# A graph-attention kernel, first layer: key tiles made of 64 keys from each of two chunks

## The chip, the cores and the metric

The kernel runs on one core of a Trainium2 chip. The metric is the time on the device in microseconds (us). Engines are named as in the profile: PE is TensorE's matmul, PEld its weight load, DVE is VectorE, ACT is ScalarE, POOL is GpSimd, SP is SyncE, which here only issues DMAs.

## The reference

Eight inputs `x[b]` of 2048 rows by 256 features pass through two layers, all in f32, with one `adj` of 2048 x 2048 for all. Each layer normalises `x`, applies a ReLU to get `h`, and adds its result to `x`. The first layer is the one that is changed:

```python
q = (h @ Wq.T + bq).reshape(B, N, H, Dh).transpose(0, 2, 1, 3)      # H = 4 heads, Dh = 64
...
kc = k.reshape(B, H, Nc, CHUNK, Dh)                                  # Nc = 8 chunks of 256 keys
vc = v.reshape(B, H, Nc, CHUNK, Dh)
scores = jnp.einsum('bhnd,bhjcd->bhnjc', q, kc) / sqrt(Dh)
scores = jnp.clip(scores, -10.0, 10.0)
scores = jnp.where(mask == 0, -10.0, scores)
attn = softmax(scores, axis=-1)                                      # within each chunk of 256 keys
ctx = jnp.einsum('bhnjc,bhjcd->bhnd', attn, vc)                      # the chunks' contexts are added
out = ctx @ Wo.T + bo
out = layernorm(out + h) * gamma + beta
```

What matters: the softmax is taken within each chunk of 256 keys. A chunk's weights are divided by their own sum before the contexts of the eight chunks are added. The second layer is another attention over the same rows, with scores `e_src[i] + e_dst[j]` and one softmax over all 2048 keys.

## The kernel before, in words

**Steps.** The first layer is a written-out sequence of 256 steps: 8 inputs (`b`, called batches), 4 blocks of 512 queries (`qb`), 8 chunks of keys (`c`). A step handles all four heads of one chunk. Its 256 keys are two key tiles of 128 (`kt`), with keys on the partitions and queries along the free axis. The loop at the end of `layers` runs over `n` and works on three steps at once: contexts of step `n`, sums of step `n + 1`, scores of step `n + 2`. Instructions go to each engine in the order in which this Python code emits them, and each engine takes its queue in that order.

**What a step does.**

- `scores` (L436): for a key tile and a pair of heads (`hp`), two matmuls with 64 features on the rows and 128 keys on the columns write a pair of PSUM banks (`pair()`, three pairs in rotation, tile name `big`). DVE clips and masks them in one instruction (L449) into a weight tile `E` (ten of them in rotation). `exponential` (L455) on ACT makes the weights in place. There are four such tiles of 128 x 1024 per step.
- `added` in `prepared` (L776): POOL adds the two key tiles, once for each pair of heads, so that one matmul per head sums a chunk.
- `add_up` (L472): four matmuls with a 128 x 32 matrix of ones, 512 queries each, put each head's sums on 32 partitions. `divide` (L479) copies them on ACT; a DMA spreads them over 128 partitions (`got`). `spread` (L486) takes reciprocals on DVE and sends them through DRAM to `r` (L488, L491: one DMA to DRAM, four back, each for 32 partitions).
- `weigh` (L461): the contexts. Four heads stand beside each other as 128x32 tiles; a head's 64 features are two halves (`part`) in two PSUM banks (`both`). Both key tiles of the chunk accumulate there.
- `accumulate` (L499, L501): DVE multiplies each bank with `r` into `c`, or straight into `acc` for a query block's first chunk; POOL adds `c` to `acc`.

**Side work.** Beside the steps, generators do the rest. `batch` and `block` make the next input's keys, values and queries: `statistics` (L47, L48), `normal`, `turn` (L157), then `narrow` matmuls (L154). `limits` makes the masks from `adj` during the first batch. `finish` closes a query block once its eight chunks are in: output projection, residual (L535), second normalisation (L544, L553), storing. `advance` lets these generators go on at its place in a step, at most one matmul item per call; the numbers in `TURN` and in the dictionary in `block` say from which step on an item may go. A generator that yields `False` is not due yet. `finish` and `statistics` are in `quiet`, which only some calls of `advance` serve.

**PSUM.** The eight banks are three pairs, for scores, sums and side work alike, and the two banks of `both`. A score tile waits for a free pair, that is for the DVE instruction that read the pair's last content.

**After the first layer** the second one runs 512 rounds with its own loop (matmuls at L847 and L858, DVE at L837, POOL at L1060, ACT at L1019). Its work is not changed but for the order of keys within a block of 512. In its very last rounds `last_ending` (L914, L929, L930) does on DVE what `ending` (L977 to L986) does on ACT and POOL for all passes before.

Of the kernel before, what the change touches and what calls it, by code (L numbers as in the profile page):

```python
# [13 lines left out]
ALU = mybir.AluOpType  # L14
# [37 lines left out]
def layers(  # L52
# [99 lines left out]
    def narrow(to, lhsT, rhs, start, stop):  # L152
        for j in range(0, P, 32):
            nc.tensor.matmul(to[j : j + 32], lhsT[:, j : j + 32], rhs, start=start, stop=stop)  # L154
# [23 lines left out]
    def sides(rhs, two, hT):  # L178

        ps = aux().rearrange("p (t f) -> p t f", t=2)  # L180
        for u in range(2):
            t = 2 * two + u
            for ic in range(FC):
                narrow(
                    ps[:, u, :],
                    hT[:, ic, t * P : (t + 1) * P],
                    rhs[:, ic, :],
                    start=(ic == 0),
                    stop=(ic == FC - 1),
                )  # L190
        return ps
# [52 lines left out]

    def limits():
# [10 lines left out]
        def cast(k):  # L256

            m = masks[:, k % 2, :]
            nc.scalar.copy(m, raws[k])
# [30 lines left out]
    TURN = (1, NCH - 2, 2 * NCH - 2, 3 * NCH + 1)  # L290
# [5 lines left out]
    def block(b, blk, xb, turned, qs, ks, vs):  # L296

        def due(*slots):

            return b == 0 or here[0] >= first_of(b) + slots[blk]  # L300

        while not due(*TURN):
            yield False
        hT = big.tile([P, FC, QB], F32, tag="hT", name="hT", bufs=1)
        yield from block_turned(xb, blk, norm_of[b], hT)
# [3 lines left out]
        for name in ("qkv" if blk == 2 else "kvq"):  # L309
            while not due(*{  # L310
                "k": (0, 0, 3 * NCH - 1, 3 * NCH + 1),
                "v": (0, 0, 3 * NCH + 1, 3 * NCH + 3),
                "q": (NCH - 2, 2 * NCH - 2, 3 * NCH - 2, 4 * NCH - 2),
            }[name]):
                yield False
            if name == "v":
                r = big.tile([P, NT, F], F32, tag="kv", name="v", bufs=12)
                for two in range(NT // 2):
                    nc.scalar.copy(r[:, 2 * two : 2 * two + 2, :], sides(wT["v"], two, hT))
                    if two == 1:  # L320
                        vs.append(r)
                    yield
                continue
            if name == "q":
# [3 lines left out]
            for oc in range(FC):  # L328
                ps = aux()
# [15 lines left out]
    def batch(b):  # L345
# [11 lines left out]
        def statistics():  # L357

            for blk in range(NQB):
                while (  # L360
                    here[0] < first_of(b) + TURN[blk] - 2 or len(turned) < blk
                    if b
# [5 lines left out]
                yield from slot()  # L368
                for t in range(NT):
                    row_stats(nc, small, mv[:, blk * NT + t, :], xb[:, t, :])  # L370
# [16 lines left out]
    for name, w in (("q", Wq), ("k", Wk), ("v", Wv), ("o", Wo)):  # L387
# [4 lines left out]
        if name == "o":  # L392

            got = big.tile([P, FC, F], F32, tag="c", name="w_halves")
            for oc in range(FC):
                nc.vector.tensor_copy(
                    got[:, oc, :].rearrange("p (s h d) -> p h s d", s=2, h=H),
                    raw[:, oc, :].rearrange("p (h s d) -> p h s d", s=2, h=H),
                )
            raw = got  # L400
# [19 lines left out]
    for s in range(2):  # L420
        for h in range(H):
            f0 = h * DH + 32 * s
            nc.sync.dma_start(bv_col[32 * h : 32 * h + 32, s : s + 1], bv[f0 : f0 + 32].unsqueeze(1))
# [12 lines left out]
    def scores(qb, kt, hp, qs, ks):  # L436

        ps = pair()
        for hh in range(2):
            own = slice(hh * DH, (hh + 1) * DH)  # L440
            nc.tensor.matmul(  # L441
                ps[:, hh, :],
                ks[kt // NT][own, hp, (kt % NT) * P : (kt % NT + 1) * P],
                qs[qb][own, hp, :],
                start=True,
                stop=True,
            )
        e = weights_of.tile([P, 2, QB], F32, tag="E", name="E")
        nc.vector.scalar_tensor_tensor(  # L449
            e, ps, -0.5, bcast(limit[:, qb, kt, :], 1, 2), ALU.max, ALU.min  # L450
# [6 lines left out]
    def weigh(kt, part, es, vs, both, first):  # L457

        for h in range(H):
            mine = slice(h * DH + 32 * part, h * DH + 32 * part + 32)  # L460
            nc.tensor.matmul(  # L461
                both[part][32 * h : 32 * h + 32, :],
                vs[kt // NT][:, kt % NT, mine],
                es[h // 2][:, h % 2, :],
                start=first,
                stop=not first,
            )

    def add_up(es, sums):

        for h in range(H):
            nc.tensor.matmul(  # L472
                sums[32 * h : 32 * h + 32, :], ones, es[h // 2][:, h % 2, :], start=True, stop=True
            )

    def divide(sums):

        s = big.tile([P, QB], F32, tag="s", name="s", bufs=1)
        nc.scalar.copy(s, sums)  # L479
        got = small.tile([P, 16], F32, tag="sum", name="sum")  # L480
        nc.sync.dma_start(got, s[0:P:32, :].rearrange("h (j i) -> h j i", i=16))
        return got

    def spread(got):

        nc.vector.reciprocal(got, got)  # L486
        held = dram.tile([H, QB], F32, tag="inv", name="inv", bufs=3)
        nc.sync.dma_start(held.rearrange("h (j i) -> (h j) i", i=16), got)  # L488
        r = big.tile([P, QB], F32, tag="r", name="r", bufs=1)
        for h in range(H):  # L490
            nc.sync.dma_start(r[32 * h : 32 * h + 32, :], held[h, :].partition_broadcast(32))  # L491
# [881 lines left out]
```

## Time and profile before

Three runs took 4089.37, 4090.36 and 4090.54 us; the median is 4090.36 us.

| | us |
|---|---|
| median of three runs | 4090.36 |
| the profiled execution's own time | 4098.12 |
| its span, from the first to the last instruction | 4096.3 |
| busy in the span: PE | 3989.7 |
| POOL | 3287.0 |
| DVE | 3158.6 |
| ACT | 2517.7 |
| first copy of sums (L479) | 57.9 |
| last copy of sums | 2700.5 |
| first matmul of the second layer's contexts (L847) | 2731.0 |

The profile's page lists busy times, the chain of work that ended last, and the costliest groups of instructions: line, engine, operation, tile written from tiles read, partitions x elements, count, then total busy time in us and mean duration in ns, then the engine's idle time just before them and what ended it. In a timeline, each row has its start in us from the span's start, its length, engine, line and tiles; rows of one kind are merged, with their count. PE writes two records for one f32 matmul, so a count of 8 is four matmuls. The TensorE clock that the chip granted was 0.994 of the full one as a mean over the run.

### The profile page before, as it was taken

The page shows a single profiled execution, that of the slowest core. Times are in us where ns is not written, and L with a number is a line of the kernel's source. Part 1 is how long each engine was busy: PE and PEld are TensorE (multiplying, and loading weights), DVE is VectorE, ACT ScalarE, POOL GpSimd, SP SyncE. Part 2 cuts the span into 40 slices and gives each one's busy share as a digit, 9 for nine tenths or more (in the row PEclk, how much of TensorE's full clock was granted, in tenths as well). Part 3 has the DMA queues.
Part 4 walks back from the last instruction along what each step waited for, and adds up shares of the span by engine and source line. Part 5 has one row for each costly group of instructions (what it writes and reads, how often), then busy time and mean ns, then how long its engine had stood idle before and what let it go on. Part 6 is the DMA issues. An engine that isn't in the chain of part 4 may idle for free.

```text
span 4096.3 us, 85966 instructions
## 1 busy us (share of the span) xinstructions
PE 3989.7 (97%) x34614; PEld 1484.8 (36%) x34614; DVE 3158.6 (77%) x3500; ACT 2517.7 (61%) x3579; POOL 3287.0 (80%) x1828
## 2 busy tenths in 40 slices
PE   7999999999999999999999999989999999999997
PEld 3333333333333333333333333333333333333532
DVE  5786666676677677677666667759999999999998
ACT  5655556565555555655565556746676767767566
POOL 2577788788788888888888889868778788777887
PEclk9999999999999999999999999999999999999999
DMA  3221121111211121122112112222222222222221
GB/s 115 89 77 52 51 58 57 52 49 55 58 55 50 53 67 49 47 60 60 49 54 59 54 47 62 67 72 60 73 60 62 63 73 65 63 70 56 54 55 48
DMA packets 350344, 248.40 MB, mean 61 GB/s; under 512 B 232944, under 2 KB 300272, under 8 KB 349936
## 3 DMA queue, kind: packets, MB, share of 16 engines
q1 hardware_dynamic: 343664, 223.67, 20.0%
q0 software_dynamic: 5184, 18.88, 1.2%
q8 instruction: 274, 4.49, 0.5%
q14 instruction: 134, 1.10, 0.1%
q10 hardware_dynamic: 1088, 0.26, 0.0%
HBM read 204.15 MB, written 36.18 MB: 59 GB/s over the span
## 4 chain that ended last, share of the span: by engine, by line
PE 81%; POOL 8%; ACT 4%; DVE 3%; issue 2%; DMA 1%; SPq 0%; ACTq 0%; POOLq 0%; DVEq 0%
PE big L441 19%; PE acc L847 18%; PE both L461 17%; PE big L154 10%; PE big L472 7%; PE den L858 6%; PE rest L154 3%; POOL add L776 3%; POOL t L1060 3%; POOL acc L501 2%; ACT E L455 2%; DVE e L837 1%; PE big L157 1%; PE rest L157 1%; DMA sum<-s 1%
## 5 line engine op out<-in xcount | busy, mean ns | idle before, releaser
L449 DVE SCALAR_TENSOR_TENSOR E<-big,limit 128x1024 f32<-128x1024 f32 x1024 | 1181.9, 1217 | 642.2 <-PE big L441 614.6
L776 POOL TENSOR_TENSOR add<-E 128x1024 f32<-128x1024 f32 x512 | 1204.0, 2375 | 444.9 <-PE both L461 417.3
L455 ACT ACTIVATE E<-E 128x1024 f32<-128x1024 f32 x1024 | 1056.2, 1057 | 682.4 <-DVE E L449 664.2
L837 DVE SCALAR_TENSOR_TENSOR e<-near,far,limit 128x2048 f32<-128x2048 f32 x512 | 1166.4, 2345 | 25.0 <-issue 18.3
L1060 POOL TENSOR_TENSOR t<-t,e 128x1024 f32<-128x1024 f32 x384 | 905.6, 2394 | 210.3 <-PE den L858 100.1
L847 PE MATMUL acc<-e,qn 128*32 128x512 f32 x8192 | 983.2, 595 | 12.1 <-DVE e L837 11.8
L461 PE MATMUL both<-E,v 128*32 128x512 f32 x8192 | 992.6, 594 | 0.0
L441 PE MATMUL big<-qT,kT 64*128 64x512 f32 x4096 | 958.8, 605 | 14.6 <-DVE E L449 11.1
L441 PEld LDWEIGHTS big<-qT,kT 64*128 64x128 f32 x4096 | 365.1, 186 | 586.9 <-issue 416.7
L1019 ACT ACTIVATE t<-e,quot 128x1024 f32<-128x1024 f32 x384 | 420.7, 1144 | 215.0 <-PE den L858 147.6
L501 POOL TENSOR_TENSOR acc<-acc,c 128x1024 f32<-128x1024 f32 x224 | 531.2, 2371 | 6.2 <-DVE c L499 6.2
L461 PEld LDWEIGHTS both<-E,v 128*32 128x32 f32 x8192 | 294.4, 109 | 535.8 <-issue 396.7
L847 PEld LDWEIGHTS acc<-e,qn 128*32 128x32 f32 x8192 | 289.9, 110 | 539.1 <-issue 428.5
L499 DVE TENSOR_TENSOR c<-both,r 128x512 f32<-128x512 f32 x448 | 308.7, 690 | 43.7 <-PE both L461 10.4
L472 PE MATMUL big<-add,ones 128*32 128x512 f32 x2048 | 280.4, 602 | 15.7 <-POOL add L776 4.7
L858 PE MATMUL den<-t,for_sums 128*32 128x512 f32 x1536 | 229.5, 594 | 4.7 <-POOL t L1060 4.5
L479 ACT COPY s<-big 128x512 f32<-128x512 f32 x256 | 150.2, 587 | 77.0 <-PE big L472 76.9
L858 PE MATMUL den<-e,for_sums 128*32 128x512 f32 x1024 | 150.8, 592 | 0.0
L154 PE MATMUL big<-hT,wk 128*32 128x512 f32 x1024 | 124.9, 603 | 7.1 <-ACT hT L165 5.9
L472 PEld LDWEIGHTS big<-add,ones 128*32 128x32 f32 x2048 | 49.0, 107 | 224.9 <-issue 141.9
L977 ACT ACTIVATE z<-z,dens 128x64 f32<-128x64 f32 x496 | 125.3, 337 | 1.9 <-DVE z L961 1.9
L154 PE MATMUL big<-hT,wq 128*32 128x512 f32 x1024 | 125.2, 603 | 1.1 <-ACT hT L165 0.7
(144 smaller groups left out, 3126.9 us busy)
## 6 DMA issues: line engine op xcount, KB each, us to landing
r<-inv SPq DMA_DIRECT2D x1024, 64.0 KB
x<-in_x_dram SPq DMA_DIRECT2D x96, 512.0 KB
es<-er SPq DMA_DIRECT2D x64, 512.0 KB
adj_in<-in_adj_dram SPq DMA_DIRECT2D x32, 512.0 KB
x<-o POOLq DMA_DIRECT2D x32, 512.0 KB, 3.3
xh<-x SPq DMA_DIRECT2D x128, 128.0 KB
out_dram<-xh SPq DMA_DIRECT2D x124, 128.0 KB
x<-x SPq DMA_DIRECT2D x28, 512.0 KB
```

The lines of the kernel that those rows point to most:

```text
L154: nc.tensor.matmul(to[j : j + 32], lhsT[:, j : j + 32], rhs, start=start, stop=stop)
L441: nc.tensor.matmul(ps[:, hh, :], ks[kt // NT][own, hp, (kt % NT) * P : (kt % NT + 1) * P], qs[qb][own, hp, :], start=True, stop=True,)
L449: nc.vector.scalar_tensor_tensor(e, ps, -0.5, bcast(limit[:, qb, kt, :], 1, 2), ALU.max, ALU.min)
L455: nc.scalar.activation(e, e, AF.Exp, scale=0.25 * EDGE)
L461: nc.tensor.matmul(both[part][32 * h : 32 * h + 32, :], vs[kt // NT][:, kt % NT, mine], es[h // 2][:, h % 2, :], start=first, stop=not first,)
L472: nc.tensor.matmul(sums[32 * h : 32 * h + 32, :], ones, es[h // 2][:, h % 2, :], start=True, stop=True)
L501: nc.gpsimd.tensor_tensor(acc, acc, to, ALU.add)
L776: nc.gpsimd.tensor_tensor(both, tiles[0][hp], tiles[1][hp], ALU.add)
L837: nc.vector.scalar_tensor_tensor(e, near, far[:, jt, h : h + 1], limit[:, :, jt, :], ALU.max, ALU.min)
L847: nc.tensor.matmul(acc[part][32 * blk : 32 * blk + 32, :], qn[jt // NT][:, jt % NT, own], e[:, blk, :], start=(jt == 0), stop=(jt == NKT - 1),
L858: nc.tensor.matmul(den[32 * blk : 32 * blk + 32, :], for_sums[:, jt, :], blocks[blk], start=first, stop=last,)
L1060: nc.gpsimd.tensor_tensor(ts[half], ts[half], now[:, 2 * half : 2 * half + 2, :], ALU.add)
```

## The change

A step now handles two chunks (a block of 512 keys, `blk`) for one pair of heads (`hp`), instead of one chunk for four heads. There are still 256 steps. Key tile `t` of a block holds keys `64 t` to `64 t + 63` of the block's first chunk on partitions 0 to 63, and the same keys of its second chunk on partitions 64 to 127.

- Scores: four matmuls per tile of 64 features by 64 keys, instead of two of 64 by 128.
- Contexts: 64 keys by 64 features, one PSUM bank for each chunk, two heads beside each other, accumulated over four tiles.
- Sums: POOL adds the four tiles of a step with three instructions. One matmul for each head and each half of the queries (256 columns), with a matrix `both_of` that holds ones for either chunk in its own columns, gives the sums of both chunks.
- Reciprocals: `r` holds them for two chunks, 128 x 1024 instead of 128 x 512, brought by two DMAs of 64 partitions. It now takes turns with `c` in the same two buffers.
- `accumulate`: DVE multiplies each chunk's bank with its part of `r`, and DVE also adds the products to `acc`, in one instruction of 128 x 512 for each chunk (one in all in a query block's first two steps, two in the others). POOL's addition is gone.
- Order within a step: the context matmuls of the first tile stand ahead of the scores, those of the other three after them, then the sums. Both calls of `advance` stand at the end of a step.
- Side work: new times, one item for each step. `finish` is spread over 14 steps, `statistics` takes two tiles at a time, and the addition of the output bias comes after the projection.
- Values, masks, and the second layer's key order follow the new order of keys. The output weights are no longer reordered in halves.

The diff, cut to what the text speaks of:

```diff
+    def mixed(t):
+        return [256 * c + 64 * t + r for c in range(2) for r in (0, 32)]
...
-            nc.scalar.copy(m, raws[k])
+            nc.scalar.copy(
+                m.rearrange("p (b t c r) -> p b c t r", b=2, t=NT, c=2),
+                raws[k].rearrange("p (b c t r) -> p b c t r", b=2, c=2, t=NT),
+            )
...
-    TURN = (1, NCH - 2, 2 * NCH - 2, 3 * NCH + 1)
+    TURN = (3, NCH + 3, 2 * NCH + 3, 3 * NCH + 3)
+    ITEMS = {
+        "k": (5, NCH + 5, 2 * NCH + 7, 3 * NCH + 5),
+        "v": (7, NCH + 7, 3 * NCH + 1, 3 * NCH + 7),
+        "q": (9, NCH + 9, 2 * NCH + 5, 4 * NCH + 1),
+    }
...
-    def scores(qb, kt, hp, qs, ks):
+    both_of = const.tile([P, 32], F32, tag="both_of", name="both_of")
+    nc.gpsimd.memset(both_of, 0.0)
+    for c in range(2):
+        nc.gpsimd.memset(both_of[64 * c : 64 * c + 64, 16 * c : 16 * c + 16], 1.0)
+
+    def scores(qb, blk, t, hp, qs, ks):
         ps = pair()
-        for hh in range(2):
-            own = slice(hh * DH, (hh + 1) * DH)
-            nc.tensor.matmul(
-                ps[:, hh, :],
-                ks[kt // NT][own, hp, (kt % NT) * P : (kt % NT + 1) * P],
-                qs[qb][own, hp, :],
-                start=True,
-                stop=True,
-            )
+        for c in range(2):
+            for hh in range(2):
+                own = slice(hh * DH, (hh + 1) * DH)
+                keys = 256 * c + 64 * t
+                nc.tensor.matmul(
+                    ps[64 * c : 64 * c + 64, hh, :],
+                    ks[blk][own, hp, keys : keys + 64],
+                    qs[qb][own, hp, :],
+                    start=True,
+                    stop=True,
+                )
...
-    def weigh(kt, part, es, vs, both, first):
-        for h in range(H):
-            mine = slice(h * DH + 32 * part, h * DH + 32 * part + 32)
-            nc.tensor.matmul(
-                both[part][32 * h : 32 * h + 32, :],
-                vs[kt // NT][:, kt % NT, mine],
-                es[h // 2][:, h % 2, :],
...
+    def weigh(hp, t, e, v, both):
+        for hh in range(2):
+            mine = slice((2 * hp + hh) * DH, (2 * hp + hh + 1) * DH)
+            for c in range(2):
+                own = slice(64 * c, 64 * c + 64)
+                nc.tensor.matmul(
+                    both[c][64 * hh : 64 * hh + 64, :],
+                    v[own, t, mine],
+                    e[own, hh, :],
+                    start=(t == 0),
+                    stop=(t == NT - 1),
+                )
+    def add_up(added, sums):
+        for hh in range(2):
+            for half in range(2):
+                n = 2 * hh + half
+                nc.tensor.matmul(
+                    sums[32 * n : 32 * n + 32, :],
+                    both_of,
+                    added[:, hh, half * 256 : (half + 1) * 256],
+                    start=True,
+                    stop=True,
+                )
...
-        r = big.tile([P, QB], F32, tag="r", name="r", bufs=1)
-        for h in range(H):
-            nc.sync.dma_start(r[32 * h : 32 * h + 32, :], held[h, :].partition_broadcast(32))
+        r = big.tile([P, 2, 2, 256], F32, tag="c", name="r")
+        for hh in range(2):
+            nc.sync.dma_start(
+                r[64 * hh : 64 * hh + 64].rearrange("p n c q -> p (n c q)"),
+                held[4 * hh : 4 * hh + 4, :].rearrange("n q -> (n q)").partition_broadcast(64),
+            )
...
     def accumulate(acc, both, r, first):
-        to = acc if first else heads_tile("c", "c")
-        for part in range(2):
-            nc.vector.tensor_tensor(to[:, part, :], both[part], r, ALU.mult)
-        if not first:
-            nc.gpsimd.tensor_tensor(acc, acc, to, ALU.add)
+        to = big.tile([P, 2, QB], F32, tag="c", name="c")
+        parts = [acc if first and c == 0 else to[:, c, :] for c in range(2)]
+        for c, mine in enumerate(parts):
+            nc.vector.tensor_tensor(
+                mine.rearrange("p (n q) -> p n q", n=2),
+                both[c].rearrange("p (n q) -> p n q", n=2),
+                r[:, :, c, :],
+                ALU.mult,
+            )
+        for mine in parts[first:]:
+            nc.vector.tensor_tensor(acc, acc, mine, ALU.add)
...
+    def added(tiles):
+        total = heads_tile("add", "add")
+        nc.gpsimd.tensor_tensor(total, tiles[0], tiles[1], ALU.add)
+        for e in tiles[2:]:
+            nc.gpsimd.tensor_tensor(total, total, e, ALU.add)
+        return total
...
+    FIRST = 1
     for n in range(-2, len(steps)):
...
-            contexts(0)
-        if n < NQB * NCH or qb == NQB - 1 or qb == 0 and c < NCH // 2:
-            advance(n < 0)
-        coming = prepared(steps[n + 2]) if n + 2 < len(steps) else iter(())
-        weights[n + 2] = [next(coming, None)]
+            for t in range(FIRST):
+                weigh(hp, t, weights[n][t], v, both)
+        if n + 2 < len(steps):
+            weights[n + 2] = prepared(steps[n + 2])
+        if n >= 0:
+            for t in range(FIRST, NT):
+                weigh(hp, t, weights[n][t], v, both)
         inside = -1 <= n < len(steps) - 1
         if inside:
-            sums = pair()[:, 0, :]
-            add_up(weights[n + 1][1], sums)
+            sums = pair()[:, 0, :256]
+            add_up(totals.pop(n + 1), sums)
             got = divide(sums)
-        weights[n + 2].append(next(coming, None))
+        if n + 2 < len(steps):
+            totals[n + 2] = added(weights[n + 2])
         if n >= 0:
-            contexts(1)
...
-            accumulate(accs[qb], both, r, c == 0)
+            accumulate(accs[qb][:, hp, :], both, r, blk == 0)
...
             r = spread(got)
+        if n < 0 or b < B - 1 or qb == NQB - 1 or qb == 0 and c < NCH // 2:
+            advance(n < 0)
         advance(mask_first=0 <= n < NCH)
```

## The prediction

> **What bounds the kernel now.** I read the page first: the busy shares, the chain, then the groups of the first layer.
>
> ```profile
> PE 3989.7 (97%) x34614; PEld 1484.8 (36%) x34614; DVE 3158.6 (77%) x3500; ACT 2517.7 (61%) x3579; POOL 3287.0 (80%) x1828
> ...
> PE 81%; POOL 8%; ACT 4%; DVE 3%; issue 2%; DMA 1%; SPq 0%; ACTq 0%; POOLq 0%; DVEq 0%
> ...
> L449 DVE SCALAR_TENSOR_TENSOR E<-big,limit 128x1024 f32<-128x1024 f32 x1024 | 1181.9, 1217 | 642.2 <-PE big L441 614.6
> L776 POOL TENSOR_TENSOR add<-E 128x1024 f32<-128x1024 f32 x512 | 1204.0, 2375 | 444.9 <-PE both L461 417.3
> ...
> L501 POOL TENSOR_TENSOR acc<-acc,c 128x1024 f32<-128x1024 f32 x224 | 531.2, 2371 | 6.2 <-DVE c L499 6.2
> ...
> L499 DVE TENSOR_TENSOR c<-both,r 128x512 f32<-128x512 f32 x448 | 308.7, 690 | 43.7 <-PE both L461 10.4
> L472 PE MATMUL big<-add,ones 128*32 128x512 f32 x2048 | 280.4, 602 | 15.7 <-POOL add L776 4.7
> ```
>
> TensorE is the bound and owns 81% of the chain. But the first layer's POOL groups are big, and the change touches POOL and DVE. The copies of the sums (L479), one per step, stand at 57.9, 438.4, 2407.4 and 2700.5 us for steps 0, 32, 224 and 255. So a step takes 11.89 us in the first batch (masks are made there), 10.26 in the six middle ones, 9.46 in the last. In the windows of 1433.0 to 1757.9, 32 steps, PE is busy 322.62 us, POOL 276.58, DVE 225.50: per step 10.1, 8.64 and 7.05.
>
> The third view is the timeline, of one step and of the last 20 us.
>
> ```profile
> 1197.62 2.35 POOL L776 TENSOR_TENSOR add<-E 128x1024 f32<-128x1024 f32 x1
> 1199.15 4.62 DVE L449 SCALAR_TENSOR_TENSOR E<-big,limit 128x1024 f32<-128x1024 f32 x4 [0.98 <-PE big L441]
> 1200.41 2.19 ACT L455 ACTIVATE E<-E 128x1024 f32<-128x1024 f32 x2 [3.51 <-DVE E L449]
> 1201.65 1.06 PE L472 MATMUL big<-add,ones 128*32 128x512 f32 x8
> 1203.68 1.50 DVE L499 TENSOR_TENSOR c<-both,r 128x512 f32<-128x512 f32 x2
> 1204.22 1.94 PE L154 MATMUL big<-wv,hT 128*32 128x256 f32 x32
> 1204.52 4.72 POOL L776 TENSOR_TENSOR add<-E 128x1024 f32<-128x1024 f32 x2 [4.55 <-PE both L461]
> ...
> 4080.44 1.26 POOL L985 TENSOR_TENSOR z<-z,low 128x512 f32<-128x512 f32 x1
> 4081.01 2.91 DVE L914 TENSOR_TENSOR z<-z,dens 128x512 f32<-128x512 f32 x2
> 4081.78 1.59 POOL L986 TENSOR_TENSOR xh<-xh,z 128x512 f32<-128x512 f32 x1
> ```
> ```profile
> L914 DVE TENSOR_TENSOR z<-z,dens x2: 1239/1494/1748, 4081.0 to 4082.2; 128x512 f32<-128x512 f32 x2
> ...
> L930 DVE SCALAR_TENSOR_TENSOR xh<-xh,low x2: 692/692/692, 4085.7 to 4087.0; 128x512 f32<-128x512 f32 x2
> ```
>
> L914 decides this forecast. It is the only DVE work with both inputs in SBUF that runs beside POOL. Its first instruction ends at 4082.25, 0.55 after POOL's L985 (4081.70); its second at 4083.92, 0.55 after L986 (4083.37). L986, whose kind takes 1.26 to 1.29, took 1.59: it ended 1.12 after DVE's first. The two engines took turns, a whole instruction each. L930, also two SBUF inputs but with POOL idle, took 0.69.
>
> **The change part by part, per step.**
>
> *Sums on PE.* Four f32 matmuls over 512 columns (8 records, 1.06 us) become four over 256. L154 has that shape: 32 records in 1.94, so 8 take 0.49. Saved about 0.5 us, on the path while PE bounds: 256 x 0.5 = 128.
>
> *Scores and contexts as 64x64 tiles.* No row of before has that shape. The nearest: a pair of 64x128 takes 958.8/1024 = 0.94, a quad of 128x32 takes 992.6/1024 = 0.97. A step keeps four groups of each, so I take no change; were only two tiles at work at once, each group would double.
>
> *POOL.* Two adds become three: 3 x 2.36 = 7.1. The context addition leaves it (2.07 on average). With the finishing work (L553, L517, roots) it has 8.64 - 4.72 - 2.07 + 7.1 = 8.95 us: under any step below, if nothing holds it.
>
> *DVE.* Same four L449 (4.62) and two L499 (1.50), plus two additions into acc, one in the two steps of eight that start a block: 1.75 x 0.55 to 0.69. With reciprocal 0.25, statistics (384 pairs of 0.53 over 256 steps, 0.80) and L535 (0.17) this is 8.3 to 8.6 without waiting. But each addition reads acc and c, both in SBUF. Alone it costs 0.69 (L930), beside POOL 1.24 to 1.75 with POOL instructions of 1.26 (L914). POOL's here are 2.36 long, so the upper end is 2.36 + 0.55 = 2.9. Which end holds depends on what POOL does at that moment, so I lay out a step, time 0 at DVE's first L449:
>
> - L449 ends 4.62. The exponentials start 1.26 after it (1200.41 against 1199.15) and take 1.06 each at DVE's spacing: the second ends at 3.47. POOL starts 0.13 later: adds 3.60 to 5.96, 5.96 to 8.32, then the third.
> - PE: the fourth score tile needs the buffer that the first L449 frees (1.2); with it 2.1; three context groups of 0.86 (spacing in the chain of waits, 16 records in 1.72) end at 4.7. The multiplications run 4.9 to 6.4.
> - Addition one is issued at 6.4, into POOL's second add: waits to 8.32, ends 8.87. POOL's third add has been queued since 8.32, so it goes next: 8.87 to 11.23. Addition two: 11.23 to 11.78.
> - Reciprocal, statistics, L535: 1.22. The next L449 starts at 13.0.
>
> In the two steps with one addition it is 8.87 + 1.22 = 10.1. Mean (6 x 13.0 + 2 x 10.1)/8 = 12.3, over PE's 9.65 (10.15 less 0.5): DVE becomes the bound, through the waits. Queued behind the waiting addition are the reciprocal, with SyncE's inv and r DMAs and the x loads behind those, and the next L449, for which ACT's exponentials and PE's fourth score tile wait. r lands about 1.5 + 3.3 after the reciprocal (L488 to L491 is 1205.59 to 1207.03; 512 KB, twice the bytes of now, landed in 3.3 in the x<-o row): 3.8 into the next step, for a multiplication at 4.9. Hidden with 1.1 to spare.
>
> The Trainium skill's page "GPSIMD Engine Reference", section "Engine selection", sends elementwise additions to VectorE as about twice as fast. By that alone the move is a gain and the sum is that of the first rival. The page "SBUF — State Buffer", section "Who interferes with whom", speaks against the change: it says that a Vector instruction with two SBUF inputs contends with a GpSimd instruction that reads SBUF, whatever its form, where L914 shows one form, twice.
>
> *The rest.* Ten weight tiles now have to hold 3 + 4 + 4, so the fourth L449 also waits for the second context group: 2.1 + 0.86 = 3.0, before its turn at 3.46, so nothing. The statistics, turnings and projections are the same instructions in other steps; the 0.17 to 0.80 terms above carry them. x loads pass SyncE's r DMAs several steps ahead of their use: nothing. The mask cast writes 64-element runs (1.04 now, ACT 61% busy): nothing. Weight halves and seven small bv DMAs fall away at the start, under 1 us. The second layer, from about 2731 us on, keeps its work.
>
> **Sum**, against the profiled execution's 4098.1 (span 4096.3 and 1.8 around it; the median of runs is 7.8 lower). Middle batches: (12.3 - 10.26) x 192 = 392. First batch: the 24 mask parts left cost DVE 2.4 each, 1.8 per step: (12.3 + 1.8 - 11.89) x 32 = 71. Last, without x statistics: (12.3 - 0.2 - 9.46) x 31 = 82. Together +545: 4643, and 4635 as a median. I round to 4630.
>
> **The rivals.**
>
> *No waiting that counts (faster).* If the additions cost 0.55 to 0.69, DVE has 8.3 to 8.6 of 9.65, PE stays the bound and saves 128: 3965. For it: 30% of DVE is idle, and L914 is two instances. Against: each ends 0.55 after a POOL instruction. It decides as long as the waits stay below 9.65 - 8.4 = 1.25 us per step.
>
> *POOL holds the step.* DVE's waits are hidden, but each addition delays POOL by 0.55: 8.95 + 0.96 = 9.9 per step, (9.9 - 10.26) x 192 = -70, near 4020; up to 4080 if roots and additions bunch. Against: it needs the DVE waits gone and POOL's kept.
>
> *One whole POOL add is spared (slower, less).* Either DVE's second addition goes before POOL's queued third add (13.0 becomes 10.7), or the multiplications end before 5.96, so that addition one follows POOL's first add (11.2). The margin is only 6.4 - 5.96 = 0.44. Means 10.5 to 10.9, so 4190 to 4290.
>
> *64x64 tiles run two at a time.* 8 groups x 0.9 = 7 us more per step: about 5800. Against: the 64x128 pair and the 128x32 quad both fill the array in one group's time.
>
> **How the numbers follow.** Two waits 0.55 (4450 to 4830, the likeliest's own range); one spared 0.25; no waiting 0.12; POOL 0.05; two at a time 0.03. A difference under 0.2% is what a measurement of this kernel cannot tell from none. Faster: 0.12 and 0.02 of POOL's case, 0.14; same 0.03; slower 0.83. The range goes from 4150, below the spared case, to 4830; outside stand about 0.2.
>
> **What would show it.** Right: the two-input addition on DVE, x448, has a mean of 2 to 2.7 us and often ends 0.55 after a POOL add; POOL's x768 adds have a mean above 2.375, some near 2.9; PE's share falls to 85 to 88%; PE idles before score tiles, released by DVE's L449 successor; the sums group halves to about 140 us; steps alternate near 10 and 13. Wrong: additions below 1.2 us on average, or PE still at 97%. It would also be wrong, at another step, if the 64x64 groups' busy time left 960 to 990 us.

## The result, and the profile after

| | before | after |
|---|---|---|
| median of runs, us | 4090.43 | 4623.79 (4618.69 to 4627.06, four runs) |
| profiled execution's own time, us | 4098.12 | 4624.55 |
| its span, us | 4096.3 | 4622.7 |
| copies of the sums, first to last, us | 57.9 to 2700.5 | 58.6 to 3214.6 |
| mean granted TensorE clock | 0.994 | 0.960 |

The ratio of after to before is 1.1303, with a 95% interval of 1.1284 to 1.1323. The change makes the kernel 13% slower. The first layer carries it: from first to last copy of the sums 2642.6 us became 3156.0, +513.4 of the span's +526.4.

The profile's page of after: the busy shares, the chain of waits by engine, and the groups of the first layer. The lines of the kernel are now L461 for score matmuls, L469 for clipping, L483 for contexts, L496 for sums, L514 for reciprocals, L530 for multiplications, L537 for additions, L826 and L828 for POOL's adds.

```profile
PE 4068.4 (88%) x38710; PEld 1402.1 (30%) x38710; DVE 4070.4 (88%) x3946; ACT 2503.9 (54%) x3579; POOL 3496.8 (76%) x1863
...
PE 51%; DVE 23%; DMA 11%; issue 9%; POOL 3%; SPq 1%; ACT 1%; DVEq 0%; POOLq 0%; ACTq 0%
...
L461 PE MATMUL big<-qT,kT 64*64 64x512 f32 x8192 | 1103.0, 641 | 436.8 <-DVE E L469 277.3
L828 POOL TENSOR_TENSOR add<-add,E 128x1024 f32<-128x1024 f32 x512 | 1293.3, 2526 | 40.1
L469 DVE SCALAR_TENSOR_TENSOR E<-big,limit 128x1024 f32<-128x1024 f32 x1024 | 1185.5, 1211 | 147.9 <-PE both L483 93.2
...
L826 POOL TENSOR_TENSOR add<-E 128x1024 f32<-128x1024 f32 x256 | 607.9, 2375 | 566.2 <-ACT E L475 565.8
L537 DVE TENSOR_TENSOR acc<-acc,c 128x512 f32<-128x512 f32 x448 | 970.1, 2166 | 8.8
L530 DVE TENSOR_TENSOR c<-both,r 128x512 f32<-128x512 f32 x448 | 291.0, 685 | 165.8 <-DMA r<-inv 91.7
...
L496 PE MATMUL big<-add,both_of 128*32 128x256 f32 x2048 | 163.6, 391 | 0.0
```

PE's share of the chain fell from 81% to 51%. The score matmuls stand idle for 436.8 us, mostly until DVE's L469 has freed a pair of banks (14.6 us before). L530 and L537 have the same shape, 128x512. L530 takes 685 ns, with `both` in PSUM. L537, with both inputs in SBUF, takes 2166. POOL's two kinds of adds have the same shape too: L826, which runs ahead of the additions, has the uncontended 2375; L828, which runs beside them, has 2526.

The same step in the timeline of after: DVE's rows, then POOL's, with start and length.

```profile
1524.01 4.60 DVE L469 SCALAR_TENSOR_TENSOR E<-big,limit 128x1024 f32<-128x1024 f32 x4
1529.42 1.29 DVE L530 TENSOR_TENSOR c<-both,r 128x512 f32<-128x512 f32 x2 [0.82 <-DMA r<-inv]
1530.63 5.02 DVE L537 TENSOR_TENSOR acc<-acc,c 128x512 f32<-128x512 f32 x2
1535.58 0.24 DVE L514 RECIPROCAL sum<-sum 128x16 f32<-128x16 f32 x1
1535.74 4.55 DVE L469 SCALAR_TENSOR_TENSOR E<-big,limit 128x1024 f32<-128x1024 f32 x4
```
```profile
1527.52 2.38 POOL L826 TENSOR_TENSOR add<-E 128x1024 f32<-128x1024 f32 x1 [0.37 <-ACT E L475]
1529.97 5.13 POOL L828 TENSOR_TENSOR add<-add,E 128x1024 f32<-128x1024 f32 x2
1535.06 2.80 POOL L598 TENSOR_TENSOR o<-o,x 128x1024 f32<-128x1024 f32 x1
```

Two additions, worth 1.4 us alone, fill 5.02. They end at 1535.65, 0.55 after POOL's pair of adds (1535.10). That pair takes 5.13 where it takes 4.7 to 4.8 beside no addition. And POOL's next instruction, L598, takes 2.80 where its kind took 2.40 before.

Over the whole first layer: 409 of the 448 additions last more than 1 us, and 408 of these end between 0.5 and 0.6 us after the end of a POOL instruction. 245 of POOL's 768 adds last more than 2.6 us.

### The profile page after: what moved, and what is told of

The parts are those of the page before. It is cut to its first block, busy times and chain, and to the rows that moved or that the text cites. A ratio compares the mean times of both kernels' runs of the same rounds, so it can differ in the third digit from the quotient of the medians.

```text
span 4622.7 us, 93792 instructions
## 1 busy us (share of the span) xinstructions
PE 4068.4 (88%) x38710; PEld 1402.1 (30%) x38710; DVE 4070.4 (88%) x3946; ACT 2503.9 (54%) x3579; POOL 3496.8 (76%) x1863
## 4 chain that ended last, share of the span: by engine, by line
PE 51%; DVE 23%; DMA 11%; issue 9%; POOL 3%; SPq 1%; ACT 1%; DVEq 0%; POOLq 0%; ACTq 0%
PE acc L898 15%; PE both L483 13%; PE big L461 10%; DVE acc L537 8%; DMA r<-inv 8%; PE den L909 5%; DVE c L530 4%; DVE E L469 4%; PE big L154 3%; DMA inv<-sum 3%; POOL t L1111 3%; PE rest L154 2%; DVE st L47 2%; DVE sum L514 1%; DVE e L888 1%
## 5 line engine op out<-in xcount | busy, mean ns | idle before, releaser
L461 PE MATMUL big<-qT,kT 64*64 64x512 f32 x8192 | 1103.0, 641 | 436.8 <-DVE E L469 277.3
L828 POOL TENSOR_TENSOR add<-add,E 128x1024 f32<-128x1024 f32 x512 | 1293.3, 2526 | 40.1
L469 DVE SCALAR_TENSOR_TENSOR E<-big,limit 128x1024 f32<-128x1024 f32 x1024 | 1185.5, 1211 | 147.9 <-PE both L483 93.2
L483 PE MATMUL both<-E,v 64*64 64x512 f32 x8192 | 1080.4, 630 | 23.1 <-DVE c L530 17.0
L826 POOL TENSOR_TENSOR add<-E 128x1024 f32<-128x1024 f32 x256 | 607.9, 2375 | 566.2 <-ACT E L475 565.8
L537 DVE TENSOR_TENSOR acc<-acc,c 128x512 f32<-128x512 f32 x448 | 970.1, 2166 | 8.8
L461 PEld LDWEIGHTS big<-qT,kT 64*64 64x64 f32 x8192 | 334.5, 139 | 1086.6 <-DVE E L469 493.7
L483 PEld LDWEIGHTS both<-E,v 64*64 64x64 f32 x8192 | 331.1, 143 | 685.2 <-issue 543.3
L530 DVE TENSOR_TENSOR c<-both,r 128x512 f32<-128x512 f32 x448 | 291.0, 685 | 165.8 <-DMA r<-inv 91.7
L496 PE MATMUL big<-add,both_of 128*32 128x256 f32 x2048 | 163.6, 391 | 0.0
L576 POOL TENSOR_TENSOR o<-o,ro 128x1024 f32<-128x1024 f32 x32 | 75.7, 2367 | 88.3 <-DVE o L573 88.3
L154 PE MATMUL big<-hT,wk 128*32 128x512 f32 x1024 | 126.4, 615 | 13.8 <-ACT hT L171 12.8
L154 PE MATMUL rest<-w,hT 128*32 128x256 f32 x2016 | 124.1, 387 | 10.7 <-DVE qn L775 10.7
```

What stands on the lines that cost most here:

```text
L154: nc.tensor.matmul(to[32 * j : 32 * j + 32], lhsT[:, n : n + 32], rhs, start=start, stop=stop)
L461: nc.tensor.matmul(ps[64 * c : 64 * c + 64, hh, :], ks[blk][own, hp, keys : keys + 64], qs[qb][own, hp, :], start=True, stop=True,)
L469: nc.vector.scalar_tensor_tensor(e, ps, -0.5, bcast(limit[:, qb, NT * blk + t, :], 1, 2), ALU.max, ALU.min)
L483: nc.tensor.matmul(both[c][64 * hh : 64 * hh + 64, :], v[own, t, mine], e[own, hh, :], start=(t == 0), stop=(t == NT - 1),)
L537: nc.vector.tensor_tensor(acc, acc, mine, ALU.add)
L826: nc.gpsimd.tensor_tensor(total, tiles[0], tiles[1], ALU.add)
```

## The experiments

All are edits of after unless the text says otherwise. The theory: an addition with two SBUF inputs on DVE and an add on POOL exclude each other, in turns of a whole instruction, and DVE's turns are late by a whole POOL add. Rivals: the additions are simply too much work for DVE; the late landing of `r` sets the step; the new tiles or sums cost the time.

**No additions at all (e1).**

```diff
-        for mine in parts[first:]:
-            nc.vector.tensor_tensor(acc, acc, mine, ALU.add)
```

> The additions of the products into acc are left out (acc keeps only the first product of a query block), all else as in the changed kernel. Theory, turns between DVE's two-input additions and POOL's adds: without the additions nothing waits for a turn, DVE has 7.3 us of work per step and PE bounds again at about 9.65 us, so 3960 to 4000. Rival, the doubled r transfer (its landings are 8% of the changed kernel's chain): the time stays over 4350. Rival, the 64x64 tiles or the new order of side work: it stays over 4300, with PE as busy as before in the first layer.

Measured: 4014.91 us, 0.9812 of before (0.9783 to 0.9840), 15 us over the expected range. Steps take 9.8 us on average in the middle batches (12.1 in after).

```profile
PE 3872.0 (96%) x38710; PEld 1397.6 (35%) x38710; DVE 3156.7 (79%) x3498; ACT 2505.4 (62%) x3579; POOL 3378.8 (84%) x1863
...
L826 POOL TENSOR_TENSOR add<-add,E 128x1024 f32<-128x1024 f32 x512 | 1212.2, 2368 | 40.1
```

PE is the bound again, and POOL's adds are back at 2368 ns. So the whole loss hangs on the additions, and 64x64 tiles, shorter sums, larger `r` and new order together do not make the kernel slower. The 76 us below before are not their gain alone: e1 leaves out the additions, which before does on POOL (531.2 us). This does not yet tell waiting from work.

**The second input from PSUM (e2).**

```diff
-        for mine in parts[first:]:
-            nc.vector.tensor_tensor(acc, acc, mine, ALU.add)
+        for c in range(int(first), 2):
+            nc.vector.tensor_tensor(acc, acc, both[c], ALU.add)
```

> The 448 additions stay, in their place and of their size, but their second input is the PSUM bank of the context and not the product c, so undivided contexts are added: part of the computation is changed. Theory, turns: a DVE addition with one input in SBUF does not wait for POOL; its mean falls from 2.17 to about 0.69 us and the time to 3970 to 4120 (the banks are held up to 1.4 us longer, which can cost PE some). Rival, too much work or too long a queue on DVE: the same number and size of additions keep the time near 4600.

Measured: 4150.84 us, 1.0144 of before (1.0115 to 1.0174). The groups of the page:

```profile
L828 POOL TENSOR_TENSOR add<-add,E 128x1024 f32<-128x1024 f32 x512 | 1213.0, 2369 | 40.2
L483 PE MATMUL both<-E,v 64*64 64x512 f32 x8192 | 1111.1, 598 | 80.8 <-DVE acc L537 76.2
L537 DVE TENSOR_TENSOR acc<-acc,both 128x512 f32<-128x512 f32 x448 | 305.1, 681 | 6.6
```

The same number of additions, of the same shape, on the same engine and at the same place: 305.1 us instead of 970.1, and the time falls by 473. Not one of POOL's 768 adds lasts more than 2.6 us. That is the waiting, separated from the work. The time came out 31 us over the expected range. A new wait is in the second line of the three: the additions hold the banks of `both` longer, and PE's context matmuls wait 76.2 us for that. Between this kernel and e1 lie 136 us, for DVE's own work and these banks.

**The additions on POOL (e3).** In the edit, `nc.vector` becomes `nc.gpsimd` in the line of the addition.

> The additions go back to POOL, one for each chunk, 128x512 (1.29 us each), all else as in the changed kernel. Theory, turns: DVE's waits are gone, POOL gets 8.95 + 1.75 x 1.29 = 11.2 us per step and bounds: about 4330, POOL over 95% busy in the first layer. Rival, the r transfer or the side work's order: no change from 4624.

Measured: 4431.44 us, 1.0830 of before (1.0798 to 1.0861); some 100 us more than expected. The chain by engine, and two groups:

```profile
POOL 51%; PE 32%; issue 8%; DVE 5%; ACT 3%; DMA 2%; POOLq 0%; SPq 0%; ACTq 0%; DVEq 0%
...
L530 DVE TENSOR_TENSOR c<-both,r 128x512 f32<-128x512 f32 x448 | 291.5, 687 | 692.9 <-POOL acc L537 674.4
...
L537 POOL TENSOR_TENSOR acc<-acc,c 128x512 f32<-128x512 f32 x448 | 573.8, 1281 | 18.4 <-DVE c L530 3.3
```

With three adds and the additions, POOL is the bound: steps of 11.5 us, where 11.2 were expected. A wait for `c` goes with it: POOL frees its buffers late, and DVE's multiplications stood idle 674.4 us until then. So putting the additions back on POOL is no remedy here: the adds of four tiles have taken the room they had.

**The kernel before, with its addition on DVE (e7 as two instructions, e8 as one).** Nothing else of the change is in these two.

```diff
-            nc.gpsimd.tensor_tensor(acc, acc, to, ALU.add)
+            for part in range(2):
+                nc.vector.tensor_tensor(acc[:, part, :], acc[:, part, :], to[:, part, :], ALU.add)
```

In e8 it is only `gpsimd` that becomes `vector`: one instruction of 128x1024.

> The kernel before, with one edit: its addition of c to acc goes from POOL (one of 128x1024) to DVE (two of 128x512). No 64x64 tiles, no new r transfer, no new side work. Theory, turns: the first addition, issued 6.0 us after the step's first L449, waits for POOL's first add (5.4 to 7.7), the second for POOL's second (to 10.6), then 1.2 us more: 12.4 us in seven of eight steps, in all 4480 to 4620, although POOL loses 531 us of work. Rival, something else in the change makes it slow: 4050 to 4150.

> The kernel before, with its addition of c to acc on DVE as one instruction of 128x1024. Theory, turns: one wait, to 7.7 or so, then 1.1 us and 1.2 us: 10.1 us per step, as long as PE takes now: 4050 to 4180. Rival, the amount of DVE work: the same time as with two additions of half the size, both slower than before by the same amount.

Measured: e7 4628.67 us, 1.1311 of before (1.1289 to 1.1334), 9 us over its range. e8 4239.11, 1.0356 (1.0339 to 1.0374), 59 over its range. The groups of e7, then of e8:

```profile
L502 DVE TENSOR_TENSOR acc<-acc,c 128x512 f32<-128x512 f32 x448 | 1062.8, 2411 | 0.0
```
```profile
L776 POOL TENSOR_TENSOR add<-E 128x1024 f32<-128x1024 f32 x512 | 1417.0, 2788 | 880.1 <-PE both L461 823.2
...
L501 DVE TENSOR_TENSOR acc<-acc,c 128x1024 f32<-128x1024 f32 x224 | 581.6, 2596 | 7.7
```

e7 loses as much as after without the new key tiles: moving the addition alone makes such a loss. That the two times agree to 5 us is partly chance, as their steps differ in all else. e8 has the same work in half as many instructions, and loses 148 us instead of 537. What counts is how often DVE has to wait for a turn. POOL waits in its turn too: its adds have a mean of 2788 ns there, against 2375 in before. That one wait still costs 148 us was more than expected: the room that DVE has beside PE does not hide it.

**One wide addition in after (e5).** In the six steps of eight that have two additions, one instruction of 128x1024 over the whole of `acc` takes their place.

```diff
+        if first:
+            nc.vector.tensor_tensor(acc, acc, parts[1], ALU.add)
+        else:
+            nc.vector.tensor_tensor(whole, whole, to, ALU.add)
```

> In the six steps of eight that made two additions of 128x512, DVE makes one of 128x1024 over the whole of acc: the same number of elements, one instruction, so one turn to wait for. The products of a step then also reach the other pair of heads, which changes the computation. Theory, turns: one wait for the rest of POOL's second add (to 8.32 after the step's first L469), then 1.1 us, and 1.2 us of reciprocal and statistics: about 10.6 us per step instead of 13.0, in all 4130 to 4270. Rival, the amount of DVE work sets the time: unchanged within 1% of 4624.

Measured: 4245.93 us, 1.0376 of before (1.0355 to 1.0397), within the range; steps of 10.6 us in the middle batches, as expected. The wide additions, then the narrow ones that are left:

```profile
L539 DVE TENSOR_TENSOR acc<-acc,c 128x1024 f32<-128x1024 f32 x192 | 540.5, 2815 | 6.7
...
L537 DVE TENSOR_TENSOR acc<-acc,c 128x512 f32<-128x512 f32 x64 | 135.8, 2123 | 2.2
```

The wide addition has a mean of 2815 ns; in after, two narrow ones with as many elements have twice 2166. So one turn less a step is worth 378 us here: 192 steps had two additions, 1.97 us for each.

**POOL's adds in halves (e13).** This asks whether a turn is an instruction, or lasts until POOL has run out of queued work.

```diff
-        nc.gpsimd.tensor_tensor(total, tiles[0], tiles[1], ALU.add)
-        for e in tiles[2:]:
-            nc.gpsimd.tensor_tensor(total, total, e, ALU.add)
+        for a, e in zip((tiles[0], total, total), tiles[1:]):
+            for hh in range(2):
+                nc.gpsimd.tensor_tensor(total[:, hh, :], a[:, hh, :], e[:, hh, :], ALU.add)
```

> The changed kernel with each of POOL's three adds of a step (128x1024, 2.37 us) issued as two of 128x512 (1.28 each, the size that e3's additions on POOL had), so POOL has 0.6 us more of its own work per step; DVE's additions are untouched. Theory, DVE and POOL take turns a whole instruction each: the wait shrinks with the length of POOL's instruction. Addition two waits 1.28 + 0.55 = 1.8 us and not 2.9, addition one at most as much; the x448 additions have a mean of 1.2 to 1.7 us where they had 2.17, a step with two additions is near 10.7 us, one with one addition is bound by PE or POOL near 9.7, and the time is 4200 to 4400. Rival, DVE waits until POOL has run out of queued work, however it is cut: the additions' mean stays at 2.2 or above, POOL works longer, and the time is 4620 to 4750.

Measured: 4299.38 us, 1.0490 of before (1.0465 to 1.0516), in the range of the theory. The additions and POOL's adds:

```profile
L828 POOL TENSOR_TENSOR add<-add,E 128x512 f32<-128x512 f32 x1024 | 1451.5, 1448 | 0.0
...
L537 DVE TENSOR_TENSOR acc<-acc,c 128x512 f32<-128x512 f32 x448 | 703.0, 1569 | 8.8
```

POOL has more instructions and more work of its own, and the kernel is 324 us faster than after. The usual long addition went from 2.73 us to 1.65, by the difference of a POOL add of 2.37 and one of 1.28. So DVE's turn comes, as a rule, after one POOL instruction, and does not wait until POOL has run out of them. But the rule has exceptions here: twelve of the 448 additions lasted 5.7 to 7.8 us. In the rows of one, DVE's and then POOL's, the first of the two additions starts at 1492.64 and takes 5.7:

```profile
1492.64 6.43 DVE L537 TENSOR_TENSOR acc<-acc,c 128x512 f32<-128x512 f32 x2
```
```profile
1490.36 2.53 POOL L828 TENSOR_TENSOR add<-E 128x512 f32<-128x512 f32 x2
1492.84 4.95 POOL L828 TENSOR_TENSOR add<-add,E 128x512 f32<-128x512 f32 x4
```

It ends 0.56 after POOL's last add of the step (1497.79): POOL did four more adds after the one that ran when the addition was issued, and DVE got no turn between them. In after no addition lasts more than 2.91. Why DVE is passed over in these twelve is not known.

**The reciprocal earlier (e4, e9).** If the late landing of `r` set the step, an earlier reciprocal would help. e4 sends it ahead of the multiplications, and writes the products over `r` itself, to have the buffers:

```diff
+            old = r
+            if inside:
+                r = spread(got)
-            accumulate(accs[qb][:, hp, :], both, r, blk == 0)
+            accumulate(accs[qb][:, hp, :], both, old, blk == 0)
...
-        if inside:
+        elif inside:
             r = spread(got)
```

e9 puts it between multiplications and additions:

```diff
-            accumulate(accs[qb][:, hp, :], both, r, blk == 0)
+            adding = accumulate(accs[qb][:, hp, :], both, r, blk == 0)
+            next(adding)
...
+        if n >= 0:
+            next(adding, None)
```

> The reciprocal and its transfers are issued ahead of the multiplications and additions of the step; the products are written over r in place, so that buffers do not lock. Theory, turns: r lands some 5 us earlier and the multiplications' waits for it (244 us idle before L530) go, but the additions still follow POOL's second and third add: 4560 to 4640. Rival, the r transfer sets the step: the time falls by 150 us or more, below 4470.

> The reciprocal and its transfers are issued between the multiplications and the additions of a step, instead of after the additions. Theory, turns: r lands 3 to 4 us earlier and the multiplications stop waiting for it, but the additions keep their turns, one after POOL's second add and one after its third, so the step ends where it did: 4560 to 4640. Rival, the r transfer sets the step: below 4470.

Measured: e4 4947.39 us, 1.2091 of before (1.2056 to 1.2126); e9 4668.99, 1.1414 (1.1391 to 1.1437). Both are over their ranges, by 307 and 29 us, and slower than after. The reciprocals of e4, then the reciprocals and additions of e9:

```profile
L514 DVE RECIPROCAL sum<-sum 128x16 f32<-128x16 f32 x256 | 64.7, 253 | 865.8 <-DMA sum<-s 865.8
```
```profile
L538 DVE TENSOR_TENSOR acc<-acc,c 128x512 f32<-128x512 f32 x448 | 688.5, 1537 | 6.6
...
L514 DVE RECIPROCAL sum<-sum 128x16 f32<-128x16 f32 x256 | 64.8, 253 | 406.4 <-DMA sum<-s 406.4
```

e4 says little about `r`: the reciprocal that was moved up stood in DVE's queue waiting for the sums' own DMA, 865.8 us, with the multiplications behind it. In e9 that wait is 406.4. But e9 does what it was made for: DVE's wait for `r` ahead of the multiplications falls from 156.0 us to 16.5. (The 244 us in e4's expectation are all of the idle time there; 156.0 are those for `r`.) The steps do not get shorter (12.1 to 12.8 us in the middle batches). Only 209 additions last more than 1 us, but 207 of these still end 0.5 to 0.6 us after a POOL instruction, and the 406.4 us of waiting for the sums are new. So the wait for `r` could be taken away without a gain; whether it would be worth something once the reciprocal does not wait for the sums, these two do not tell.

**The additions later (e6).** Those of a step are issued between the second and the third L469 of the next.

```diff
+            owed.append((acc, mine))
...
+            tiles.append(scores(qb, blk, t, hp, qs, ks))
+            if t == 1:
+                pay()
```

> The two additions of a step are issued later, between the second and the third L469 of the next iteration, 2.3 us after its first L469, where POOL has finished the last step's adds and not yet begun the next ones (1.05 to 3.6 after it), but for steps with finishing work on POOL. Same instructions, same sizes, same result. Theory, turns: no wait in half of the steps, one or two in those with finishing work; mean step 10.5 to 11, in all 4170 to 4340, mean of the additions about 1 us. Rival, the amount of DVE work: no change from 4624, as the work is the same.

Measured: 4375.51 us, 1.0693 of before (1.0671 to 1.0714), 36 us over the range. The additions' mean is 1126 ns, and 290 of the 446 in the trace take about 0.7 us. In the timeline these fall where POOL does its roots or waits for the exponentials. But the finishing work's adds on POOL (128x1024, 2.38) lie there too: one such pair of additions took 4.92, with the third L469 queued behind it. A better place in the order avoids part of the waits, not all. A new wait came with it: the reciprocal, which no longer stands behind the additions, waits 503.5 us in all for the sums' DMA (9.1 in after). What that adds to the time is not told by this run; in e1 such waits come to 355.2 us, with PE as the bound.

**Products back into their PSUM banks (e10), and the first contexts after the second score tile (e12).** e10 leaves each product in the bank that it was made from, so that each addition has one PSUM input. e12 does this too, and moves the first tile's contexts behind two of the four score tiles, so that the banks may be freed later; `prepared` yields after two score tiles.

```diff
-        to = big.tile([P, 2, QB], F32, tag="c", name="c")
-        parts = [acc if first and c == 0 else to[:, c, :] for c in range(2)]
+        parts = [acc if first and c == 0 else both[c] for c in range(2)]
```
```diff
+        coming = prepared(steps[n + 2]) if n + 2 < len(steps) else iter(())
+        next(coming, None)
+        if n >= 0:
             for t in range(FIRST):
                 weigh(hp, t, weights[n][t], v, both)
         if n + 2 < len(steps):
-            weights[n + 2] = prepared(steps[n + 2])
+            weights[n + 2] = next(coming)
```

> The products are written back into the PSUM banks of the contexts, and the additions take them from there: same result, same number and size of additions, one SBUF input each. Theory, turns: no addition waits for POOL (mean 0.69 us); as in the run whose additions read the contexts from PSUM, 4130 to 4180. Rival: writing to PSUM costs DVE or holds the banks longer than that run showed, over 4250.

> As the kernel with products in PSUM, and the first tile's contexts stand after the second score tile and not ahead of the first, so that PE has 1.8 us more of other work before it needs the banks that the additions hold. Theory: of the about 136 us by which PSUM additions stay above no additions at all, PE's waits for the banks (76 us) go: 4060 to 4110. Rival, DVE's own work of 0.69 us for each addition is on the path: no gain, 4130 to 4180.

Measured: e10 4127.86 us, 1.0096 of before (1.0079 to 1.0113), 2 us below its range. e12 4020.96, 0.9829 (0.9812 to 0.9845), 39 below its range: 1.7% less than before, and 603 us less than after. The groups of e10, then of e12:

```profile
L483 PE MATMUL both<-E,v 64*64 64x512 f32 x8192 | 1106.8, 597 | 64.8 <-DVE acc L536 61.8
...
L536 DVE TENSOR_TENSOR acc<-acc,both 128x512 f32<-128x512 f32 x448 | 306.0, 683 | 8.8
```
```profile
PE 3872.2 (96%) x38710; PEld 1362.9 (34%) x38710; DVE 3440.7 (86%) x3946; ACT 2500.4 (62%) x3579; POOL 3379.4 (84%) x1863
...
L483 PE MATMUL both<-E,v 64*64 64x512 f32 x8192 | 998.7, 591 | 11.1 <-DVE acc L536 9.7
L529 DVE TENSOR_TENSOR both<-both,r 128x512 f32<-128x512 f32 x448 | 293.3, 694 | 142.3 <-DMA r<-inv 80.5
L536 DVE TENSOR_TENSOR acc<-acc,both 128x512 f32<-128x512 f32 x448 | 305.9, 683 | 8.8
```

The product into PSUM costs no more than into SBUF (694 ns against 685). The additions take 683, beside a POOL as busy as ever. What was left in e10, PE waiting 61.8 us for the banks, is 9.7 in e12, and e12 stands 6 us from e1, which adds nothing. DVE's 1.2 us of additions per step are then covered by steps of 9.75 us (middle batches), as long as e1's. DVE still waits 80.5 us for `r` there; it costs little while PE is the bound.

## Why the prediction was right

It gave 4630 us for 4623.79 measured; the likeliest case, two waits, is what happened. That the forecast is only 6 us off is luck: the terms below miss by +35, +9, -11 and -12 us, and taking 7.8 off for the median (the profiled run of after lies 0.8 above it) and rounding did the rest.

- *Turns of a whole instruction, from two rows of L914.* Shown. In the step above, with 0 at DVE's first L469 (1524.01), the prediction had POOL's three adds end at 5.96, 8.32 and 11.23 and the second addition at 11.78. The trace has 5.88, 8.33, 11.10 and 11.64. e2 and e13 show that neither the additions' work nor POOL's share sets this, but the length of one POOL instruction, with the twelve exceptions of e13, which the prediction's rule does not cover. The condition of the rival "one add spared" (multiplications ending before 5.96) was not met: they ended at 6.7.
- *Steps.* Predicted 10.1 with one addition and 13.0 with two. Averaged by place in the group of eight, over the middle batches, the two with one addition take 10.4 and 10.1, the others 11.7 to 13.6, 12.7 on average. The step shown takes 11.73, as it carries no statistics. Their 1.22 was spread evenly in the sum, but lies in some steps only.
- *Sum by batches.* First 14.44 us per step (14.1 predicted), middle ones 12.12 (12.3), last 11.82 (12.1). This is (14.44 - 11.89) x 32 + (12.12 - 10.26) x 192 + (11.82 - 9.46) x 31 = 82 + 357 + 73 = 512 us, against 71 + 392 + 82 predicted. The middle is 35 too high, the last 9 too high, the first 11 too low. Some 12 us of the span's growth lie after the last copy of the sums; the prediction had none there, and no run followed them up.
- *What it would show.* Additions: 2166 ns, within 2 to 2.7 us. POOL's adds: 2476 as a mean of the 768, the longest 2.89. PE 88% busy. PE idle until L469: shown.
- *`r` hidden with 1.1 us to spare.* Wrong in size. Its landing took 3.9 to 6.4 us in the 82 places where the chain of waits has it (3.98 for the one that follows the reciprocal shown at 1535.58), not 3.3, and the multiplications wait for it in 114 of the 256 steps, 156.0 us in all. It did not move the sum much, because what comes next, an addition, waits for POOL's turn anyway: in the step shown PE's contexts end at 4.93, so without the wait the multiplications could start at most 0.5 earlier than at 5.41, and the first addition would be issued at 6.1 instead of 6.62, still into POOL's second add (5.96 to 8.33). The trace has the same in most of the 114 steps: in 93 the first addition ended behind a POOL instruction that would have been running already if the multiplications had not waited for `r` (an estimate that leaves POOL's times as they are). In the other 21 the wait for `r` may have counted. No run settles it: e9, with almost no wait for `r`, is no faster, but has a new wait in its place.
- *Sums.* 163.6 us in place of 280.4, so 117 saved and not 128. In after's first layer PE is not the bound, so this cannot show in full; in e1 it may be part of the 76.
- *64x64 tiles at no change.* The text named 960 to 990 us as the sign, and the groups left that band: 1103.0 and 1080.4. By its own sign this step was wrong, though most of that is the waiting and not the shape. The median record is 589 ns, as for the 64x128 pair before (589), and in e1 the two groups have 969.6 and 1016.0, in e12 1022.1 and 998.7: together 34 and 69 us more than the 1951.4 before. So "no change" holds to 2 to 4%. The longer records of after go with the granted clock of 0.95 in the middle batches (1433 to 1758 us), where PE is 85% busy; in the same window before, PE is 99% busy at 1.00. In after the two groups are busy 198 us longer than in e1; how much of the loss comes by way of these longer records is not separated by any run.
- *The Trainium skill.* "GPSIMD Engine Reference", section "Engine selection", was right on the single instruction: 681 ns on DVE in e2 against 1281 on POOL in e3. Alone it would have misled on the time. "SBUF — State Buffer", section "Who interferes with whom", named what mattered: its rule on a Vector instruction with two SBUF inputs agrees with the long additions of after (408 of 409 behind a POOL instruction), and so does the exception for one input, in 448 additions of e2, e10 and e12 each.

## What to carry to other kernels

Before moving work to an engine that has room, look where its inputs lie and what its neighbour does at that moment: in this kernel 0.7 us of DVE work took 2.2 with both inputs in SBUF beside a busy POOL. Count such instructions and not their elements: one wide addition for two took 378 us off, POOL's adds in halves 324, and one input left in PSUM 473 (e2) or, with the result of the change kept, 496 (e10). Where an operand is made from a PSUM bank, write it back into that bank, and then give the banks the time that this takes, by moving PE's next use of them.

## What these runs show of the hardware

- The long additions of after end 0.5 to 0.6 us after a POOL instruction, 408 times in 409, and POOL then has to wait in its turn (adds of 2.7 for 2.37). The prediction had this from two rows. In after the two engines alternate, even when POOL has its next instruction queued; with POOL's adds in halves (e13), twelve additions of 448 were passed over for several POOL instructions in a row.
- The cost of a wait does not depend much on DVE's width: 2815 ns for 128x1024 against 2123 for the 128x512 additions of the same kernel (e5, in other steps), 0.69 apart, about the 0.68 that one more addition of 512 columns takes without a wait.
- A product over its own input in PSUM runs at 694 ns, 128x512, and costs DVE nothing beyond the 685 of a product into SBUF.
- A PE that is kept waiting was also granted less clock: 0.95 at 85% busy in after, 1.00 at 99% in before (1433 to 1758 us). The two do not fall in step: in the same window of e4 it is 0.97 at 81%.
